# The output projection of an attention by Strassen's seven products, in a three-layer kernel on one Trainium2 core

## The chip, the cores and the metric

The kernel runs on one core of one Trainium2 chip. A core has five engines that work side by side, each through its own list of instructions in a fixed order: TensorE (PE in the profile) multiplies matrices into PSUM, VectorE (DVE) and ScalarE (ACT) do elementwise work, GpSimd (POOL) does some of it too and issues the indirect transfers, SyncE (SP) issues the other transfers. An instruction can wait for semaphores that other engines or transfers raise; what stands behind it in the same list then waits too.

The metric is the device time of one execution in microseconds (us), as the median of several runs. A profiled execution is one run of its own; its time and its span (first to last instruction) are given beside the median.

## The reference

The input is 4 images of 16 x 16 positions with 1024 channels, 1024 tokens in all, in float32. Three layers follow each other, each added to its input:

```
x = x + conv_hybrid(group_norm(x))        # linear attention with relative positions
t = t + attention(layer_norm(t))          # 16 heads of 64, causal, 256 tokens per image
t = t + ffn(layer_norm(t))                # 8 experts of 1024 x 1024, gated by a softmax
```

The part that matters here is the end of the second layer and the start of the third:

```
y = einsum('bhqk,bhkd->bhqd', att, v).transpose(0, 2, 1, 3).reshape(B, T, C)
t = t + einsum('btc,oc->bto', y, W_proj) + b_proj
...
x = layer_norm(t)
gate_logits = softmax(x @ gate_w + gate_b)
weights = gate_logits * (gate_logits >= 0.1), normalised to sum 1
out = sum over e of weights[:, e] * (x @ expert_w[e] + expert_b[e])
```

The projection multiplies 1024 tokens x 1024 channels by a 1024 x 1024 matrix.

## The kernel before

**Tiles and names.** Tokens lie in 8 tiles of 128 rows (NT). A contraction over 1024 channels is 8 matmuls of 128 x 128 stationary by 128 x 512 moving, added up in one PSUM bank; HALF is 512. y_T is the attention's result with channels on the partitions, so its 128-token columns serve as the stationary operand. w_p holds W_proj's transpose in two halves of its output columns, w_p[0] and w_p[1]. xs (named xb in the profile) are the rows of the residual stream; x_rows is where they wait in DRAM while the attention runs.

**The attention's steps.** Heads go in 8 pairs, images in 4 batches: 32 steps (pair, b). In step i the loop turns the softmax of step i - 2 (`turned`, L619, L620), does products of the query and key projection (`project_qk`, L491), multiplies by the values (`values`, L629, L636) and computes the next scores (`scores`: matmuls at L575 into the one PSUM buffer `sc`, then L583 on DVE, the maxima L595, exponentials L597 on ACT, reciprocal L604, multiplication L607 on POOL). From step 28 the projection's first pieces take the place of `project_qk`: `out_at` gives tiles 0 to 2, one half each step.

**Strassen in the kernel.** `project_v`, `project_qk` and the experts' `products` already use the Winograd form with seven products: for 2 x 2 blocks A and B, `sums_of_A` (L150 to L153) forms three sums and, in place of a21, a fourth; three more sums T and one in place of b12 are formed of B. For the attention the sums of B are formed of ln1, which lies in the buffer `big1`; its last reader is the product (7, 3) in step 27.

**The projection.** `project_out(t, j, halfway)` does the 8 matmuls of tile t and half j (L648) and one DVE addition of the bank into xs[t] (L651). After the fourth matmul and after the eighth it calls `halfway`, which starts pieces of the third layer's preparation.

**The gating.** For each tile `stage(n, t)` has four parts: `normalise` (statistics L840 and L842, reciprocal root L131 to L133, the normalised row L846, its transposes L828 on PE, evicted by ACT at L832 and DVE at L834, and a copy by_quarter L850 that SP writes to `rows`); `gate` (matmuls L862 and L866 and a softmax over 8 experts in small DVE instructions, L873 to L885); `place` (matmuls L892 and L893, the position in each expert's list, L900 to L907, entries on POOL or, for the last two tiles, DVE at L915); and `enter` (matmuls L926). The table `after` says behind which half of a piece each stage of each tile is called. `normalise` writes its row into a tile with the tag `ye` (three buffers), by_quarter into the tag `xg` (two).

**The first expert.** `w0` is loaded once the projection's earlier weights are done with. A block under `tc.manual_schedule()`, whose order is the order of the text, begins with `first_sum(0)` and `second_sum(0)` (L1046, L1049: T of 128 x 2048, in a pool `t_pool` of their own), `bias_step` (L1053), the gathers of the first rows (L718, POOL) and a dense product (`weighted`, L739) for the last tile of tokens.

**What sets the order.** Outside that block a scheduler with its own cost estimates orders each engine's list ahead of time; the tile pools decide which buffer a tile takes and so what its first writer has to wait for. PSUM banks come under two tags with three buffers each: `mm` and `tr`; the transposes and the gating's results use `tr`.

Of the kernel before, what the change touches and what calls it, by code (L numbers as in the profile page):

```python
# [32 lines left out]
F32 = mybir.dt.float32  # L33
# [6 lines left out]
P = 128  # L40
# [27 lines left out]
def kernel(  # L68
# [29 lines left out]
    def pool(stack, name, bufs=1, **kw):  # L98
        return stack.enter_context(tc.tile_pool(name=name, bufs=bufs, reuse_waits="tile", **kw))
# [10 lines left out]
    def big_tile(n, name, shape=(NC, TOK)):  # L110
        return big[n].tile([P, *shape], F32, tag="big", name=name)

    def w_tile(name, *parts, home=None):

        w = (home or wpool).tile([P, NC, HALF], F32, tag="w", name=name)
        at = 0
        for part in parts:
            n = part.shape[1]
            nc.sync.dma_start(w[:, :, at : at + n], part.rearrange("(c p) n -> p c n", p=P))
            at += n  # L120
        return w
# [335 lines left out]
    with ExitStack() as attention:  # L457
# [180 lines left out]
        project_v(0)  # L638
        project_v(1)
        y_T = big_tile(0, "y_T")  # L640
        w_p = []

        def project_out(t, j, halfway=lambda: None):
            if not w_p:
                w_p.extend(w_tile(f"w_p{j}", W_projT[:, ts(j, HALF)]) for j in range(2))
            po = mm(f"po{t}_{j}")
            for c in range(NC):
                nc.tensor.matmul(po, y_T[:, c, ts(t, P)], w_p[j][:, c, :], start=(c == 0), stop=(c == NC - 1))  # L648
                if c == NC // 2 - 1:
                    halfway()  # L650
            nc.vector.tensor_add(xs[t][:, ts(j, HALF)], xs[t][:, ts(j, HALF)], po)  # L651
# [11 lines left out]
        units[22].remove((6, 5))  # L663
        units[23] = [(6, 5)]
        units.update({24: [(7, 1), (7, 2), (7, 6)], 25: [(7, 7), (7, 4)], 26: [(6, 3), (7, 5)], 27: [(7, 3)]})
        out_at = {28: (0, 0), 29: (1, 0), 30: (2, 0), 31: (0, 1), 32: (1, 1), 33: (2, 1)}
        for n in order:
            project_qk(0, n)
        soft = {}
        for i in range(len(steps) + 2):  # L670
            if i >= 2:
                s_T = turned(*steps[i - 2], soft.pop(i - 2))
            for unit in units.get(i, ()):
                project_qk(*unit)
            if i == 27:
                sums.close()
                x_pool = pool(x_home, "xb", side="right")
                xs = [x_pool.tile([P, C], F32, tag=f"x{t}", name=f"xb{t}") for t in range(NT)]
                for t in range(NT):
                    nc.sync.dma_start(xs[t], x_rows[ts(t, P), :])  # L680
            if i in out_at:
                project_out(*out_at[i])
            if i >= 2:
                values(*steps[i - 2], s_T)
            if i < len(steps):
                soft[i] = scores(*steps[i])


    left.close()

    rows = dram.tile([TOK, C], F32, name="rows")
    table = rows.rearrange("t (f c) -> (t f) c", f=Q)
# [7 lines left out]


    weights = ExitStack()
    w_even, t_pool = pool(weights, "w_even", 2), pool(weights, "t_pool")

    def half_weights(e, r, home, name="w_e"):

# [25 lines left out]

    def weighted(gate, row_T, w, bias, home, name, between={}):

        y = home.tile([P, C], F32, tag="ye", name=f"{name}_ye", bufs=3)
        for j in range(2):
            pe = mm(f"{name}_pe{j}")
            for c in range(NC):
                nc.tensor.matmul(pe, row_T[:, c, :], w[j][:, c, :], start=(c == 0), stop=(c == NC - 1))  # L739
            between.get(j, lambda: None)()  # L740
            nc.vector.tensor_add(y[:, ts(j, HALF)], pe, bias[:, ts(j, HALF)])
            nc.scalar.mul(y[:, ts(j, HALF)], y[:, ts(j, HALF)], gate)
        return y
# [36 lines left out]
    with ExitStack() as gating:  # L780
# [55 lines left out]
        def normalise(t):  # L836

            stats = small.tile([P, 2, 6], F32, tag="ln_stats", name=f"ln2_stats{t}")
            for j in range(2):
                nc.vector.bn_stats(stats[:, j, :], xs[t][:, ts(j, HALF)])  # L840
            mv = small.tile([P, 2], F32, tag="ln_mv", name=f"ln2_mv{t}")
            nc.vector.bn_aggr(mv, stats)  # L842
            rstd = small.tile([P, 1], F32, tag="ln_rstd", name=f"ln2_rstd{t}")
            inverse_root(rstd, mv[:, 1:2], EPS)
            row = l2w.tile([P, C], F32, tag="ye", name=f"row{t}", bufs=3)
            nc.vector.tensor_scalar(row, xs[t], mv[:, 0:1], rstd, ALU.subtract, ALU.mult)  # L846
            row_T = l2w.tile([P, NC, P], F32, tag="row_T", name=f"row_T{t}", bufs=3)
            transpose_rows(row, row_T, f"row{t}")
            by_quarter = l2w.tile([P, Q, C // Q], F32, tag="xg", name=f"by_quarter{t}")
            nc.scalar.copy(  # L850
                by_quarter.rearrange("p f (c i) -> p c f i", c=NC),
                row.rearrange("p (c f i) -> p c f i", c=NC, f=Q),
            )
            nc.sync.dma_start(rows[ts(t, P), :], by_quarter.rearrange("p f c -> p (f c)"))
            return row_T
# [109 lines left out]
            nc.vector.tensor_copy(add[:, a:b, :], slot[:, a:b, 0, :])  # L965

        w0 = [half_weights(0, r, w_even) for r in range(2)]
        bias0 = expert_bias(0, l2w)


        turned_rows, gated, placed = {}, {}, {}
# [1 line left out]
        def stage(n, t):  # L973
# [8 lines left out]
                enter(t, *placed[t])  # L982


        pieces = [(t, j) for t in range(3, NT) for j in range(2)]
        after = {
            0: (0, 2, 4, 6),
            1: (2, 4, 6, 8),
            2: (4, 6, 8, 10),
            3: (6, 8, 10, 12),  # L990
            4: (9, 11, 13, 15),
            5: (13, 14, 16, 17),
            6: (17, 18, 21, 23),
            7: (20, 22),
        }
        halves = 0

# [5 lines left out]
                        stage(n, t)  # L1003
            halves += 1

        for piece in pieces:
            project_out(*piece, halfway)
            halfway()
        while halves < 24:
            halfway()  # L1010
        read_lists(0, 1, copy_lists(0))

# [29 lines left out]
            return w[e][l][:, 4 * j : 4 * j + 4, :]  # L1042

        def first_sum(e):
            T[e] = [t_pool.tile([P, NC // 2, HALF], F32, tag=f"T{i}", name=f"T{i}_{e}") for i in range(3)]
            nc.vector.tensor_sub(T[e][0], half(e, 0, 1), half(e, 0, 0))  # L1046

        def second_sum(e):
# [9 lines left out]
        def third_sum(e):  # L1058
# [5 lines left out]
                last_rows.append(free[:, NC // 2 : NC // 2 + 2, :].rearrange("p a b -> p (a b)"))  # L1064
            nc.vector.tensor_sub(T3[e], half(e, 0, 1), half(e, 1, 1))

        row = {}
        last = SLOTS // P

# [62 lines left out]
        def left_over(e):  # L1132

            d = e - 1
            between = {0: lambda: (fourth_sum(e), put(e, 1), get(e, 3)), 1: lambda: row_sums(e, 0)}
            get(e, 2)
            y_d, y_e = (l2w.tile([P, C], F32, tag="ye", name=f"left{e}_{i}", bufs=3) for i in range(2))

            for j in range(2):
                bank = (tr if j else mm)(f"left{e}_{j}")  # L1140
                for c in range(NC):
                    a = A[d, last][:, c, :] if j == 0 or c < NC // 2 else A[d, "sum"][:, c - NC // 2, :]
                    for i in range(Q):
                        stationary, of = (a[:, ts(i, 32)], d) if i < Q - 1 else (A[e, last][:, c, 64:LEFT], e)
                        nc.tensor.matmul(  # L1145
                            bank[ts(i, 32), :], stationary, w[of][j][:, c, :], start=(c == 0), stop=(c == NC - 1)
                        )
                between[j]()
                y = y_d[:LEFT, ts(j, HALF)]
# [182 lines left out]
```

## Time and profile before

| what | value |
|---|---|
| median of 3 runs | 1291.41 us (1291.14 to 1291.78) |
| the profiled execution: its time | 1290.33 us |
| the profiled execution: its span | 1288.5 us |
| mean granted PE clock | 0.994 |
| PE busy | 1266.1 us, 98% of the span |
| DVE busy | 670.3 us, 52% |
| ACT busy | 248.7 us, 19% |
| POOL busy | 336.7 us, 26% |
| projection's matmuls, L648 | 647.3 to 789.8 us, 116.1 us busy |
| rows of the projection's result added, L651 | 16 of 128 x 512, 685 ns each |
| half-clock stretches | 304.79 to 308.20, 792.90 to 799.72, 837.27 to 840.68 us |

Lines of the timeline read: start, length, engine, line of the kernel, operation, what is written and read, how many; in brackets the idle time of that engine just before, and what ended it. A matmul in float32 appears as two records, so eight records are four matmuls. Records of PE overlap: a run's length has a tail in which the next one has already begun.

### The profile page before, as it was taken

To read this page: it belongs to the slowest core of one execution; us is meant where nothing else is said; L and a number is where in the kernel's file an instruction comes from. 1 tells how busy PE (TensorE), PEld (TensorE's weight loads), DVE (VectorE), ACT (ScalarE), POOL (GpSimd) and SP (SyncE) were. 2 spreads that over 40 slices of the span, in tenths; PEclk is the share of its full clock that TensorE was granted. 3 is DMA by queue.
4 is the path that set the end of the run, shared out by engine and by line. 5 is a ranking of instruction groups with operands and counts; after the bars stand their busy time and mean duration, and the time that the engine had idled before them with its cause. 6 is when DMAs were issued, how large, how long until landed. Compare 5 with 4: busy or idle time off the path is not lost.

```text
span 1288.5 us, 12902 instructions
## 1 busy us (share of the span) xinstructions
PE 1266.1 (98%) x4838; PEld 676.3 (52%) x4838; DVE 670.3 (52%) x1265; ACT 248.7 (19%) x578; POOL 336.7 (26%) x359
## 2 busy tenths in 40 slices
PE   9999999998999999999999998999999999999998
PEld 5444895787884455555454554444344434433443
DVE  5884210566322555555344745655656565665642
ACT  3300111230000333334223322011111011111110
POOL 0000060230000211222121010553644555263520
PEclk9999999999999999999999998999999999999999
DMA  9020022612202202010323515365667475557442
GB/s 353 4 66 15 3 70 65 243 66 82 66 1 65 66 1 66 1 66 1 112 85 98 198 50 199 95 177 129 157 175 224 99 235 131 160 108 220 98 82 51
DMA packets 60563, 134.58 MB, mean 104 GB/s; under 512 B 5808, under 2 KB 20160, under 8 KB 60496
## 3 DMA queue, kind: packets, MB, share of 16 engines
q1 hardware_dynamic: 47664, 94.32, 20.8%
q0 software_dynamic: 12832, 39.39, 13.9%
q8 instruction: 40, 0.66, 0.2%
q14 instruction: 27, 0.22, 0.1%
HBM read 96.72 MB, written 32.77 MB: 100 GB/s over the span
## 4 chain that ended last, share of the span: by engine, by line
PE 93%; DVE 4%; DMA 1%; POOL 1%; issue 1%; ACT 0%; DVEq 0%; POOLq 0%; ACTq 0%
PE p L1103 29%; PE pqk L491 15%; PE po L648 8%; PE pq L259 7%; PE pv L491 7%; PE left L1145 3%; PE pT L378 3%; PE py L443 2%; PE pk L321 2%; PE pc L342 2%; PE pv L403 2%; PE sc L575 2%; PE pst L619 2%; PE pa L629 2%; PE rest L1159 2%; PE last_pe L1257 1%
## 5 line engine op out<-in xcount | busy, mean ns | idle before, releaser
L718 POOL DMA_INDIRECT w_e_xg<-rows,gather x146 | 156.1, 1069 | 67.4 <-issue 40.5
L1103 PE MATMUL p<-w_e,A 128*128 128x512 f32 x368 | 164.9, 598 | 1.8 <-DVE slot L964 1.8
L607 POOL TENSOR_TENSOR s<-s,total 128x256 f32<-128x256 f32 x64 | 51.6, 827 | 345.3 <-DVE total L604 345.3
L1103 PEld LDWEIGHTS p<-w_e,A 128*128 128x128 f32 x368 | 70.2, 192 | 91.5 <-issue 91.1
L648 PE MATMUL po<-w_p,y_T 128*128 128x512 f32 x256 | 116.1, 598 | 0.0
L1103 PE MATMUL p<-T,S 128*128 128x512 f32 x256 | 112.7, 593 | 0.0
L1109 ACT ACTIVATE y<-y,slot 128x512 f32<-128x512 f32 x64 | 46.0, 722 | 340.6 <-DVE y L1117 185.6
L746 POOL DMA_INDIRECT out_dram<-y,add x32 | 57.0, 1782 | 175.5 <-ACT y L1109 114.2
L259 PE MATMUL pq<-w_q,xn 128*128 128x512 f32 x224 | 99.6, 596 | 1.4 <-DVE q_s L263 1.1
L491 PE MATMUL pqk<-ln,w_qk 128*128 128x512 f32 x192 | 85.0, 592 | 0.0
L1103 PEld LDWEIGHTS p<-T,S 128*128 128x128 f32 x256 | 48.6, 190 | 60.8 <-issue 60.7
L648 PEld LDWEIGHTS po<-w_p,y_T 128*128 128x128 f32 x256 | 46.3, 190 | 49.1 <-issue 48.7
L728 DVE STREAM_TRANSPOSE A<-w_e_xg 128x1024 f32<-128x1024 f32 x32 | 39.6, 1239 | 58.4 <-DMA w_e_xg<-rows,gather 58.4
L259 PEld LDWEIGHTS pq<-w_q,xn 128*128 128x128 f32 x224 | 41.8, 190 | 51.8 <-issue 47.4
L597 ACT ACTIVATE s<-s,top 128x256 f32<-128x256 f32 (+1 forms) x128 | 56.6, 443 | 18.0 <-DVE top L595 18.0
L491 PEld LDWEIGHTS pqk<-ln,w_qk 128*128 128x128 f32 x192 | 35.9, 190 | 42.1 <-issue 41.1
L620 ACT COPY s_T<-pst 128x384 f32<-128x384 f32 x64 | 27.5, 481 | 157.6 <-PE pst L619 157.6
L491 PE MATMUL pqk<-T,S_qk 128*128 128x512 f32 x128 | 57.7, 593 | 0.0
L1103 PE MATMUL p<-w_e,S 128*128 128x512 f32 x128 | 57.5, 592 | 0.0
L1103 PE MATMUL p<-T,A 128*128 128x512 f32 x128 | 57.5, 592 | 0.0
L491 PE MATMUL pv<-w_v,ln 128*128 128x256 f32 x192 | 43.8, 381 | 0.0
L1145 PE MATMUL left<-w_e,one 128*32 128x512 f32 x312 | 41.8, 593 | 0.0
(266 smaller groups left out, 1818.5 us busy)
## 6 DMA issues: line engine op xcount, KB each, us to landing
w_e<-in_expert_w_dram SPq DMA_DIRECT2D x16, 2048.0 KB, 12.4
w_qk<-in_W_attnT_dram SPq DMA_DIRECT2D x8, 1024.0 KB, 5.2
xn<-in_xT_dram SPq DMA_DIRECT2D x8, 512.0 KB, 7.9
x_at<-in_x_dram SPq DMA_DIRECT2D x8, 512.0 KB, 8.0
w_v<-in_W_attnT_dram SPq DMA_DIRECT2D x2, 2048.0 KB
x_rows<-x_at SPq DMA_DIRECT2D x8, 512.0 KB, 2.6
w_p<-in_W_projT_dram SPq DMA_DIRECT2D x2, 2048.0 KB, 7.6
xb<-x_rows SPq DMA_DIRECT2D x8, 512.0 KB, 6.0
```

The source lines that it names most:

```text
L259: nc.tensor.matmul(pq, xn[:, c, ts(t, P)], w_q[kc][:, c, :], start=(c == 0), stop=(c == NC - 1))
L378: nc.tensor.matmul(out_T[:, g, :, :], window[:, kc, :, :].rearrange("p i j -> p (i j)"), q0[:, kc, first : first + n_i, nj, :], start=(kc ...
L491: nc.tensor.matmul(bank, stationary(c), moving(c), start=(c == 0), stop=(c == NC // 2 - 1))
L597: nc.scalar.activation(s[:, h, cols], s[:, h, cols], AF.Exp, bias=top[:, qt, h : h + 1], accum_out=total[:, qt, h : h + 1],)
L607: nc.gpsimd.tensor_mul(s[:, :, cols], s[:, :, cols], total[:, qt, :].unsqueeze(2).to_broadcast([P, 2, (qt + 1) * P]),)
L648: nc.tensor.matmul(po, y_T[:, c, ts(t, P)], w_p[j][:, c, :], start=(c == 0), stop=(c == NC - 1))
L718: nc.gpsimd.indirect_dma_start(out=row[:, g, :], out_offset=None, in_=table[: (TOK - P) * Q, :] if e in SHORT else table, in_offset=bass.I ...
L728: nc.vector.transpose(row_T[:, :, :slots].rearrange("p c (g j) -> p g c j", j=32), row[:, : slots // 32, :].rearrange("p g (c i) -> p g c ...
L746: nc.gpsimd.indirect_dma_start(out=out[: TOK - P, :] if e in SHORT else out, out_offset=bass.IndirectOffsetOnAxis(ap=add[:slots, e, k : k ...
L1103: nc.tensor.matmul(bank, a[:, c, :], b[:, c, :], start=(c == 0), stop=(c == NC // 2 - 1))
L1109: nc.scalar.mul(y[i][:, ts(j, HALF)], y[i][:, ts(j, HALF)], slot[:, e, 1, 2 * pair + i : 2 * pair + i + 1])
L1145: nc.tensor.matmul(bank[ts(i, 32), :], stationary, w[of][j][:, c, :], start=(c == 0), stop=(c == NC - 1))
```

## The change

The projection of the first six tiles is done in three pairs of tiles. A pair's 256 x 1024 block of y is cut into 2 x 2 blocks (tile by half of the contraction), w_p into 2 x 2 blocks (half of the contraction by half of the outputs), and seven products of four matmuls give the four blocks of the result. `out_sums` forms the sums of w_p once, three of them in `big1` (where ln1 was), one in place of b12; `pair_sums` forms a pair's sums of y, with the fourth in place; `project_pair` does one product and its additions into xs. Tiles 6 and 7 keep the eight matmuls per half; as b12 no longer holds the weights, the second half's last four matmuls use `tile_sum`, the sum of both halves of y.

The sums use 15 of the 16 pieces of `big1`; so `big1` is kept to the end (`left.close()` goes), and the experts' T then lie there (`t_e`) instead of in `t_pool`. The tag `ye` gets two buffers for three, and the first expert's bias takes an `xg` buffer. The table `after` is written anew for the new order of pieces.

```diff
-        def project_out(t, j, halfway=lambda: None):
-            if not w_p:
-                w_p.extend(w_tile(f"w_p{j}", W_projT[:, ts(j, HALF)]) for j in range(2))
+        def out_sums():
+            nonlocal t_p, s_p, u_p
+            w_p.append(w_tile("w_p1", W_projT[:, HALF:]))
+            flat = big_tile(1, "out_sums").rearrange("p a b -> p (a b)")
+            t_p = [flat[:, ts(i, 4 * HALF)].rearrange("p (c n) -> p c n", n=HALF) for i in range(3)]
+            s_p = [flat[:, ts(12 + i, HALF)] for i in range(3)]
+            u_p = flat[:, ts(15, HALF)]
+            b11, b12, b21, b22 = (w_p[l][:, 4 * j : 4 * j + 4, :] for j in range(2) for l in range(2))
+            nc.vector.tensor_sub(t_p[0], b12, b11)
+            nc.vector.tensor_sub(t_p[1], b22, t_p[0])
+            nc.vector.tensor_sub(b12, b12, b22)
+            nc.vector.tensor_sub(t_p[2], b21, t_p[1])
...
+        def pair_sums(pair):
+            blocks = (y_T[:, 4 * j : 4 * j + 4, ts(2 * pair + i, P)] for i in range(2) for j in range(2))
+            sums_of_A(*blocks, *(by_tile(a) for a in s_p))
+
+        def tile_sum(t):
+            nc.vector.tensor_add(by_tile(s_p[t % 2 * 2]), y_T[:, :4, ts(t, P)], y_T[:, 4:, ts(t, P)])
+
+        def project_pair(pair, n):
...
+            a, b = {
+                1: (a11, b11),
+                2: (a12, b21),
+                3: (s4, b22),
+                4: (a22, t_p[2]),
+                5: (s1, t_p[0]),
+                6: (s2, t_p[1]),
+                7: (s3, t3),
+            }[n]
+            bank = (tr if n in (3, 5, 6) else mm)(f"po{pair}_{n}")
+            for c in range(NC // 2):
+                nc.tensor.matmul(bank, a[:, c, :], b[:, c, :], start=(c == 0), stop=(c == NC // 2 - 1))
+
+            u2, u3 = u_p, s_p[1]
+            if n == 1:
+                nc.scalar.copy(u2, bank)
+                nc.vector.tensor_add(c11, c11, bank)
+            elif n == 2:
+                nc.vector.tensor_add(c11, c11, bank)
+            elif n == 3:
+                nc.vector.tensor_add(c12, c12, bank)
+            elif n == 6:
+                nc.vector.tensor_add(u2, u2, bank)
+                nc.vector.tensor_add(c12, c12, u2)
+            elif n == 7:
+                nc.vector.tensor_add(u3, u2, bank)
+                nc.vector.tensor_add(c22, c22, u3)
+            elif n == 5:
+                nc.vector.tensor_add(c12, c12, bank)
+                nc.vector.tensor_add(c22, c22, bank)
+            else:
+                nc.vector.tensor_add(c21, c21, bank)
+                nc.vector.tensor_add(c21, c21, u3)
+
+        def project_out(t, j, halfway):
             po = mm(f"po{t}_{j}")
             for c in range(NC):
-                nc.tensor.matmul(po, y_T[:, c, ts(t, P)], w_p[j][:, c, :], start=(c == 0), stop=(c == NC - 1))
+                y = by_tile(s_p[t % 2 * 2])[:, c - 4, :] if j and c >= 4 else y_T[:, c, ts(t, P)]
+                nc.tensor.matmul(po, y, w_p[j][:, c, :], start=(c == 0), stop=(c == NC - 1))
...
-        out_at = {28: (0, 0), 29: (1, 0), 30: (2, 0), 31: (0, 1), 32: (1, 1), 33: (2, 1)}
+        out_order = [(pair, n) for pair in range(3) for n in (1, 2, 3, 6, 7, 5, 4)]
...
+            if i == 25:
+                w_p.append(w_tile("w_p0", W_projT[:, :HALF]))
             if i == 27:
+                out_sums()
                 sums.close()
...
-            if i in out_at:
-                project_out(*out_at[i])
+            out_units = out_order[2 * (i - 28) : 2 * (i - 27)] if i >= 28 else []
+            if i == 28:
+                pair_sums(0)
+            for unit in out_units[:1]:
+                project_pair(*unit)
             if i >= 2:
                 values(*steps[i - 2], s_T)
+            if i == 31:
+                pair_sums(1)
+            for unit in out_units[1:]:
+                project_pair(*unit)
...
-    left.close()
-    w_even, t_pool = pool(weights, "w_even", 2), pool(weights, "t_pool")
+    w_even = pool(weights, "w_even", 2)
...
-        y = home.tile([P, C], F32, tag="ye", name=f"{name}_ye", bufs=3)
+        y = home.tile([P, C], F32, tag="ye", name=f"{name}_ye", bufs=2)
...
-            row = l2w.tile([P, C], F32, tag="ye", name=f"row{t}", bufs=3)
+            row = l2w.tile([P, C], F32, tag="ye", name=f"row{t}", bufs=2)
...
-        bias0 = expert_bias(0, l2w)
...
         after = {
             0: (0, 2, 4, 6),
-            1: (2, 4, 6, 8),
-            2: (4, 6, 8, 10),
-            3: (6, 8, 10, 12),
-            4: (9, 11, 13, 15),
-            5: (13, 14, 16, 17),
-            6: (17, 18, 21, 23),
-            7: (20, 22),
+            1: (1, 3, 5, 7),
+            2: (3, 5, 7, 9),
+            3: (5, 7, 9, 11),
+            4: (9, 11, 13, 14),
+            5: (11, 12, 14, 15),
+            6: (14, 15, 18, 20),
+            7: (17, 19),
         }
...
-        for piece in pieces:
-            project_out(*piece, halfway)
+        for pair, n in out_order[12:]:
+            if (pair, n) == (2, 1):
+                pair_sums(2)
+            project_pair(pair, n)
             halfway()
-        while halves < 24:
+        for t in range(NT - 2, NT):
+            tile_sum(t)
+            for j in range(2):
+                project_out(t, j, halfway)
+                halfway()
+        bias0 = expert_bias(0, l2w, tag="xg", bufs=2)
+        while halves < 21:
             halfway()
...
         def first_sum(e):
-            T[e] = [t_pool.tile([P, NC // 2, HALF], F32, tag=f"T{i}", name=f"T{i}_{e}") for i in range(3)]
+            T[e] = t_e
             nc.vector.tensor_sub(T[e][0], half(e, 0, 1), half(e, 0, 0))
...
+        t_e = big_tile(1, "t_e").rearrange("p a b -> p (a b)")
+        t_e = [t_e[:, ts(i, 4 * HALF)].rearrange("p (c n) -> p c n", n=HALF) for i in range(3)]
```

More of the change, by code (lines that the diff above doesn't have):

```diff
@@ L640 @@
         y_T = big_tile(0, "y_T")
-        w_p = []
-        def project_out(t, j, halfway=lambda: None):
-            if not w_p:
-                w_p.extend(w_tile(f"w_p{j}", W_projT[:, ts(j, HALF)]) for j in range(2))
+        w_p, t_p, s_p, u_p = [], None, None, None
+        def out_sums():
[10 more added lines that the diff above has]
+            nc.vector.tensor_sub(t_p[2], b21, t_p[1])
@@ new lines, in by_tile @@
+        def by_tile(a):
+            return a.rearrange("p (c n) -> p c n", n=P)
+        def pair_sums(pair):
[4 more added lines that the diff above has]
+        def project_pair(pair, n):
+            a11, a12, s3, a22 = (
+                y_T[:, 4 * j : 4 * j + 4, ts(2 * pair + i, P)] for i in range(2) for j in range(2)
+            )
+            b11, t3, b21, b22 = (w_p[l][:, 4 * j : 4 * j + 4, :] for j in range(2) for l in range(2))
+            s1, s2, s4 = (by_tile(a) for a in s_p)
+            c11, c12, c21, c22 = (xs[2 * pair + i][:, ts(l, HALF)] for i in range(2) for l in range(2))
+            a, b = {
[30 more added lines that the diff above has]
+                nc.vector.tensor_add(c21, c21, u3)
@@ L982, in stage @@
                 enter(t, *placed[t])
-        pieces = [(t, j) for t in range(3, NT) for j in range(2)]
         after = {
             0: (0, 2, 4, 6),
-            1: (2, 4, 6, 8),
-            2: (4, 6, 8, 10),
-            3: (6, 8, 10, 12),
-            4: (9, 11, 13, 15),
-            5: (13, 14, 16, 17),
-            6: (17, 18, 21, 23),
-            7: (20, 22),
+            1: (1, 3, 5, 7),
[5 more added lines that the diff above has]
+            7: (17, 19),
         }
@@ L1136, in left_over @@
             get(e, 2)
-            y_d, y_e = (l2w.tile([P, C], F32, tag="ye", name=f"left{e}_{i}", bufs=3) for i in range(2))
+            y_d, y_e = (l2w.tile([P, C], F32, tag="ye", name=f"left{e}_{i}", bufs=2) for i in range(2))
             for j in range(2):
```

## The prediction

> **What bounds the kernel now.** I read the page first (busy time, then the chain that ended last), then the two stages that the change touches, then the places where TensorE (PE) waits.
>
> ```profile
> span 1288.5 us, 12902 instructions
> ...
> PE 1266.1 (98%) x4838; PEld 676.3 (52%) x4838; DVE 670.3 (52%) x1265; ACT 248.7 (19%) x578; POOL 336.7 (26%) x359
> ...
> PE 93%; DVE 4%; DMA 1%; POOL 1%; issue 1%; ACT 0%; DVEq 0%; POOLq 0%; ACTq 0%
> ...
> L648 PE MATMUL po<-w_p,y_T 128*128 128x512 f32 x256 | 116.1, 598 | 0.0
> ```
>
> PE is busy 98% of the span and 93% of the chain, so a PE instruction that goes is time, unless a wait takes its place. L648 is the output projection, with no idle time before it. One matmul shows as two records, so x256 is 128 matmuls.
>
> The next fence is busy time by stage: the end of the attention, the projection with the gating, and, from the third line on, four stretches of 3.41 us. The number after the five engines is the granted PE clock.
>
> ```profile
> 645.00:705.00 60.00, 60.00 (x238) 29.98 (x238) 25.70 (x62) 18.60 (x57) 11.82 (x19) 1.00 0.20 75
> 705.00:790.00 85.00, 83.56 (x453) 42.09 (x452) 50.50 (x200) 26.28 (x36) 7.21 (x12) 1.00 0.32 119
> 833.86:837.27 3.41, 1.46 (x5) 0.93 (x6) 3.09 (x13) 0.00 (x0) 0.00 (x0) 1.00 0.00 0
> 837.27:840.68 3.41, 3.41 (x6) 1.33 (x5) 3.05 (x5) 0.25 (x1) 0.00 (x0) 0.50 0.02 5
> 792.90:796.31 3.41, 2.85 (x20) 2.73 (x20) 1.28 (x5) 1.63 (x2) 0.00 (x0) 0.50 1.04 398
> 796.31:799.72 3.41, 3.41 (x19) 1.21 (x12) 2.25 (x10) 0.00 (x0) 0.00 (x0) 0.50 1.03 389
> ```
>
> The reader is to see two things: VectorE (DVE) is 43% and 59% busy in the first two stages, and a stretch in which PE was busy for 1.46 of 3.41 us is followed by one at half clock. Last, the places where PE or DVE waits, or where the order matters, in order of time:
>
> ```profile
> 645.02 0.69 DVE L567 TENSOR_TENSOR qk<-pqk,U_qk 128x512 f32<-128x512 f32 x1 [0.51 <-PE pqk L491]
> ...
> 646.76 0.96 DVE L583 SCALAR_TENSOR_TENSOR s<-sc,mask 128x768 f32<-128x768 f32 x1 [0.44 <-PE sc L575]
> ...
> 650.16 0.18 DVE L604 RECIPROCAL total<-total 128x4 f32<-128x4 f32 x1 [1.40 <-ACT s L597]
> ...
> 650.51 1.61 POOL L607 TENSOR_TENSOR s<-s,total 128x256 f32<-128x256 f32 x2 [4.21 <-DVE total L604]
> ...
> 655.05 0.92 PE L575 MATMUL sc<-qk 64*128 64x256 f32 x8
> ...
> 706.61 1.09 PE L828 MATMUL row_pt<-ident,row 128*128 128x128 f32 x8 [1.21 <-DVE row L846]
> ...
> 718.93 2.29 DVE L1046 TENSOR_TENSOR T<-w_e,w_e 128x2048 f32<-128x2048 f32 x1 [0.49 <-DMA w_e<-in_expert_w_dram]
> ...
> 721.14 0.15 DVE L883 TENSOR_TENSOR g_top<-g_top,g_fix 128x1 f32<-128x1 f32 x1
> ...
> 781.75 3.60 PE L648 MATMUL po<-w_p,y_T 128*128 128x512 f32 x8
> ...
> 789.81 0.69 DVE L651 TENSOR_TENSOR xb<-xb,po 128x512 f32<-128x512 f32 x1
> ...
> 792.50 0.81 DVE L846 TENSOR_SCALAR row<-xb,ln_mv,ln_rstd 128x1024 f32<-128x1024 f32 x1
> ...
> 793.46 1.94 PE L828 MATMUL row_pt<-ident,row 128*128 128x128 f32 x8 [3.68 <-DVE row L846]
> ```
>
> PE waits 3.68 us for the last tile's normalised row, and 1.21 us for tile 0's.
>
> **1. PE work that goes: -10.3 us.** Before, 8 tiles x 2 halves x 8 = 128 matmuls. After, 3 pairs x 7 products x 4 = 84, and tiles 6 and 7 keep 32: 116. A run of 4 (x8 records) shows 3.60 us with its tail; 16 records issue in 6.97 us (647.28 to 654.25, the next instruction's start), so 4 take 3.44 and the 12 that go 3 x 3.44 = 10.3. All lie on PE's chain. Bounds: 10.0, and 10.9 by the page's busy time (24 x 116.1 / 256).
>
> **2. Sums of the weights in front of a softmax: +4.2 us.** out_sums puts four 128x2048 subtractions on DVE. Their length is L1046's: 2.29, and 2.21 to the next start (718.93 to 721.14). The first overwrites ln1's buffer, so it waits for the last product that reads ln1, which is the one that L567 at 645.02 evicts. In the built program's DVE list stand, in this order: L567, the first sum, one y_T eviction (0.40 to the next start), the other three sums, and only then L583 for the scores that PE computed at 645.7. So L583 moves from 646.76 to 645.71 + 4 x 2.21 + 0.40 = 654.95. Two waits follow on PE. The scores have one PSUM buffer: the next L575, due at 655.05, waits for L583's end at 655.9 (0.9). Then PE's list holds the transposes of those late scores. Before, POOL's first product began 3.75 us after L583; now three more pair sums (L151 to L153, 0.69 each) also stand in front of L604: L583 654.95, L150 655.85, L595 to 657.5, three sums to 659.5, POOL at 659.85, its first block done at 660.5, while PE is free at 656.9: about 3.3 us. Before, the same transposes had 3.5 us in hand. Behind L583 on DVE wait only evictions that have PSUM buffers left. Bounds: 0.9 (only the first wait) and 6 (the next L583, also some 4 us late, adds part of its lateness).
>
> **3. The clock after that wait: +1.5 us.** 833.86 to 837.27 shows that a stretch with 1.9 us of PE idle time costs half the clock in the next 3.41 us. With 0.9 and 3.3 us idle, little more than a score product apart, some stretch has as much wherever its borders lie. Half of 3.41 is 1.7; as part of it can fall in the wait itself I take 1.5, with 0 and 3.4 (two stretches, as at 792.90 and 796.31) as bounds. [...]
>
> **4. First stage of the gating: -1.2 us.** PE waited 1.21 us for tile 0's row, because DVE did 3.7 us of constants (701.96 to 705.66) after the last attention matmul. Now two products, 6.9 us, stand on PE between the two, where 4.6 us stood. Bounds -1.2 and 0.
>
> **5. Evictions and sums on DVE: +0.6 us.** Before, 16 additions of 0.69 (L651). After, 3 x 11 + 4 = 37, three sets of four pair sums and two tile sums of 0.69 each. With the weights' sums the first stage goes from 25.7 to about 49 us (9.1 + 8 x 0.69 + 12 x 0.69 more) of some 65, the second from 50.5 to 56 (4.6 of T goes, 15 x 0.69 comes) of 75: three quarters in both. So the cover is DVE's last quarter and the two sets of PSUM buffers. Laid out with these lengths, one product (pair 1's sixth) waits 0.2 for its sum, and one list matmul 0.4 for POOL. Bounds 0 and 6.3 (0.3 for each of 21 products; rival A). ACT's three copies (L832's 0.59) have room in 18.6 of 60.
>
> **6. The first expert's sums land on the path: +4.2 us.** first_sum(0) and second_sum(0) (L1046, L1049) ran at 718.93 and 721.88 beside PE's work. Now T lies where out_sums lay, and the last half of tile 7's projection still reads a tile sum there. In the built DVE list the first sum stands right behind tile 7's last L651, ahead of its statistics, and the second between the statistics and L846. So the wait at 793.46 grows by 2 x 2.21, less 0.2 of the square root's round trip that the second sum covers. Nothing else is on PE then. The half clock that follows (792.90 to 799.72) stays, with 1.7 either way for where the stretches fall; I take 0. Behind L846, gating, lists and the POOL gathers from 803.01 shift as a block.
>
> **At nothing.** w_p's second half still waits for its buffer (issued 629.6, 7.6 us to landing) and is needed at 645.7. w_e's first loads now wait for the last read of v1 instead of ln1; they are needed 60 us later. The bias load (9.4 us to landing) moves on SP behind tile 6's copy, some 15 us ahead of its use; expert 1's now also waits for the last row's transfer (2.6), with expert 2's weights behind it, which wait for expert 0's products anyway. Two row buffers for three: rows come in pairs some 20 us apart, and a copy takes 1.04. POOL's order of work is unchanged.
>
> **Sum:** -10.3 + 4.2 + 1.5 - 1.2 + 0.6 + 4.2 = -1.0. The profiled execution took 1290.33 (span 1288.5); 1.0 less is 1289.3. The median of the runs, 1291.41, lies 1.1 above it: **1290.4**.
>
> **Rivals.** *A, slower: DVE becomes the bound of the pair products.* Each waits for a bank whose eviction stands in DVE's list behind gating work. For it: three quarters busy in strict order, and three of seven products share their buffers with the transposes and gating results. Against it: 0.3 us of slack at each of the gating's products is what the lengths leave. At 0.3 for each of 21 products, 5.7 more than step 5: 1296.1. It decides from (2.6 + 1.0) / 21 = 0.17 us a product. *B, faster: the clock.* It stays full after step 2's wait (-1.5), and the low stretch after the tail is one, not two (-1.7): 1287.2. For it: 705.24 to 706.61, with 1.21 us idle, stayed at full clock. Against: the row at 833.86. *C: the tail's sums are hidden anyway,* as at 718.93: -4.2, 1286.2; against it stands their place in the list.
>
> **How the numbers follow.** A measurement of this kernel can tell about 0.2% (2.6 us) from no change: 1288.8 to 1294.0. The forecast has 0.56 (own range 1288.4 to 1293.2, from the halves of the bounds of steps 2, 3 and 5), A 0.23, B 0.17, C 0.03, anything else 0.01. Faster: B nearly whole, C and a little of the first, 0.21; slower: A and a little of the first, 0.25; within: 0.54. The range reaches into A to 0.25 us a product (1295.4) and down to B's value: 1287.1 to 1295.4.
>
> **What would show it.** Right: the projection's matmuls take 232 records for 256; DVE's four 2.2 us subtractions at 645 to 655 with L583 behind them, and PE waiting 4 us before the next transposes, with clock 0.50 after it; no wait for tile 0's row; a wait of 7.9 us for tile 7's row with the two T sums in it. Wrong: PE waiting for DVE before pair products (A), clock 1.00 after 660 (B), a tail of 4 us (C).

## The result, and the profile after

The changed kernel takes 1290.83 us (median of 12 runs, 1289.11 to 1293.00) and the kernel before, in 12 runs, 1291.28 us (1289.79 to 1292.66). The ratio is 0.9999, with a 95% interval of 0.9990 to 1.0007: no change that can be measured. The forecast was 1290.4 us and "within 0.2%". The profiled execution took 1290.30 us against 1290.33 before, where the steps summed to -1.0.

So twelve matmuls of 0.86 us are gone and nothing is gained. The interest lies in where they went. First the page of the changed kernel: span, busy time, and shares of the chain that ended last.

```profile
span 1288.3 us, 12901 instructions
...
PE 1259.5 (98%) x4814; PEld 673.2 (52%) x4814; DVE 698.1 (54%) x1304; ACT 245.1 (19%) x577; POOL 335.2 (26%) x359
...
PE 90%; DVE 4%; issue 3%; DMA 2%; POOL 1%; ACT 0%; POOLq 0%; DVEq 0%; ACTq 0%
```

PE has 24 records fewer (4838 to 4814), which are the 12 matmuls. Its busy time fell by only 6.6 us. At half clock a matmul is busy for longer (one of the records of L687, at 661.6 us, takes 1.06 us where most take 0.59), and the changed kernel has more of those, as the clock column below shows.

Next, the waits of PE in the changed kernel, sorted by their sum: total us, times, longest.

```profile
PE row_pt L903 <- DVE row L921: 7.6, 1, 7.6
PE pv L491 <- DVE T L480: 4.0, 1, 4.0
PE pst L619 <- POOL s L607: 3.3, 1, 3.3
PE p L1186 <- DVE slot L1039: 1.8, 1, 1.8
...
PE sc L575 <- DVE s L583: 1.0, 1, 1.0
PE pn L1106 <- DVE U L1198: 0.6, 1, 0.6
```

Before, the first of these was two waits of 3.7 and 1.2 us. Now tile 0's row costs nothing and tile 7's costs 7.6. The waits of 3.3 and 1.0 us are new. They lie together, and the timeline shows why: first DVE around 646 us, then PE (start, us, engine, line, operation, output and inputs, idle time before).

```profile
645.59 0.69 DVE L567 TENSOR_TENSOR qk<-pqk,U_qk 128x512 f32<-128x512 f32 x1 [0.52 <-PE pqk L491]
646.20 2.81 DVE L653 TENSOR_TENSOR out_sums<-w_p,w_p 128x2048 f32<-128x2048 f32 x1
648.93 0.47 DVE L636 TENSOR_SCALAR y_T<-pa,bv 128x256 f32<-128x256 f32 x1
649.32 2.27 DVE L654 TENSOR_TENSOR out_sums<-w_p,out_sums 128x2048 f32<-128x2048 f32 x1
651.52 2.28 DVE L655 TENSOR_TENSOR w_p<-w_p 128x2048 f32<-128x2048 f32 x1
653.72 2.28 DVE L656 TENSOR_TENSOR out_sums<-w_p,out_sums 128x2048 f32<-128x2048 f32 x1
655.93 0.95 DVE L583 SCALAR_TENSOR_TENSOR s<-sc,mask 128x768 f32<-128x768 f32 x1
```

```profile
656.93 0.92 PE L575 MATMUL sc<-qk 64*128 64x256 f32 x8 [1.05 <-DVE s L583]
661.12 0.69 PE L619 MATMUL pst<-ident,s 128*128 128x128 f32 x2 [3.27 <-POOL s L607]
```

The softmax's scaling (L583) stands behind the four sums of the weights. PE first waits 1.05 us for the scores' only bank, and then 3.27 us for transposes of the scores that are late by the sums. Then the same places by stretches of 3.41 us (us, busy time of PE, PEld, DVE, ACT, POOL with counts; the first number after POOL is the granted clock):

```profile
653.69:657.10 3.41, 2.36 (x8) 0.82 (x8) 3.41 (x4) 0.00 (x0) 0.00 (x0) 1.00 0.00 0
657.10:660.52 3.42, 0.75 (x8) 0.51 (x8) 3.42 (x8) 1.86 (x8) 0.07 (x1) 0.98 0.00 0
660.52:663.93 3.41, 2.81 (x7) 1.68 (x8) 3.41 (x7) 0.00 (x0) 1.54 (x2) 0.50 0.00 0
663.93:667.34 3.41, 3.41 (x7) 1.58 (x6) 0.30 (x1) 2.61 (x10) 0.00 (x0) 0.52 0.00 0
667.34:670.75 3.41, 3.41 (x15) 1.55 (x14) 1.26 (x3) 0.00 (x0) 0.74 (x2) 1.00 0.00 0
...
645.00:705.00 60.00, 55.56 (x213) 27.26 (x212) 41.19 (x65) 18.30 (x58) 12.50 (x19) 0.94 0.28 98
705.00:790.00 85.00, 81.75 (x457) 41.35 (x455) 61.93 (x238) 23.47 (x34) 7.19 (x12) 1.00 0.36 134
```

The wait is followed by two stretches at half clock, where the forecast counted little less than one. The last two lines are the stages as a whole: DVE went from 25.7 to 41.2 us and from 50.5 to 61.9. It is busier, but of the pair products only one waits for it, for 0.12 us at 702 us. Last, the tail, DVE and then PE:

```profile
786.79 0.69 DVE L717 TENSOR_TENSOR xb<-xb,po 128x512 f32<-128x512 f32 x1
787.39 0.17 DVE L954 TENSOR_SCALAR g_keep<-listed 128x8 f32<-128x8 f32 x1
787.47 2.29 DVE L1127 TENSOR_TENSOR t_e<-w_e,w_e 128x2048 f32<-128x2048 f32 x1
...
790.85 2.29 DVE L1130 TENSOR_TENSOR t_e<-w_e,t_e 128x2048 f32<-128x2048 f32 x1
...
793.39 0.81 DVE L921 TENSOR_SCALAR row<-xb,ln_mv,ln_rstd 128x1024 f32<-128x1024 f32 x1
```

```profile
794.34 1.94 PE L903 MATMUL row_pt<-ident,row 128*128 128x128 f32 x8 [7.59 <-DVE row L921]
```

The two sums of the first expert's weights run between tile 7's last addition and its row, while PE waits.

The account, from marks in both profiles: from the start of L567 to the end of PE's last projection matmul passed 144.75 us before (645.02 to 789.77) and 141.16 us after (645.59 to 786.75), 3.6 less. In it are -10.3 of matmuls, +4.32 of the two waits, +3.05 of clock (6.82 us at half speed, in which PE was not waiting for 6.09) and -1.21 of tile 0's row. What remains for the evictions and everything else is +0.55. Then the wait for tile 7's row grows by 3.91 (3.68 to 7.59), the half clock behind it costs about what it did (3.0 for 3.1), and the wait at the experts' counts is 0.44 shorter. Ahead of the changed part the kernel was 0.57 later (a wait of 3.97 for 3.51 at 300 us is most of it). That is hardly the change's doing: the profile of e7, an edit of the kernel before, has 3.9 there too, and that of e1, an edit of the changed kernel, has 3.5. By this account PE's last matmul should start 0.3 later than before, and it starts 0.31 later (1282.20 for 1281.89).

### The profile page after: what moved, and what is told of

It is laid out like the page before. It is cut to its first block, busy times and chain, and to the rows that moved or that the text cites. A ratio compares the mean times of both kernels' runs of the same rounds, so it can differ in the third digit from the quotient of the medians.

```text
span 1288.3 us, 12901 instructions
## 1 busy us (share of the span) xinstructions
PE 1259.5 (98%) x4814; PEld 673.2 (52%) x4814; DVE 698.1 (54%) x1304; ACT 245.1 (19%) x577; POOL 335.2 (26%) x359
## 4 chain that ended last, share of the span: by engine, by line
PE 90%; DVE 4%; issue 3%; DMA 2%; POOL 1%; ACT 0%; POOLq 0%; DVEq 0%; ACTq 0%
PE p L1186 29%; PE pqk L491 15%; PE pq L259 7%; PE pv L491 7%; PE po L687 5%; PE left L1228 3%; PE pT L378 3%; PE py L443 2%; PE pk L321 2%; PE pc L342 2%; PE pv L403 2%; PE sc L575 2%; PE pst L619 2%; PE pa L629 2%; PE po L714 2%
## 5 line engine op out<-in xcount | busy, mean ns | idle before, releaser
L1186 PE MATMUL p<-t_e,S 128*128 128x512 f32 x256 | 112.7, 592 | 0.0
L1186 PEld LDWEIGHTS p<-t_e,S 128*128 128x128 f32 x256 | 48.6, 190 | 60.8 <-issue 60.7
L1186 PE MATMUL p<-t_e,A 128*128 128x512 f32 x128 | 57.5, 592 | 0.0
L1186 PEld LDWEIGHTS p<-t_e,A 128*128 128x128 f32 x128 | 24.4, 190 | 30.9 <-issue 30.6
L378 PE MATMUL pT<-q,window 128*128 128x256 f32 (+3 forms) x256 | 40.4, 320 | 0.0
```

Source lines behind the costliest of these rows:

```text
L378: nc.tensor.matmul(out_T[:, g, :, :], window[:, kc, :, :].rearrange("p i j -> p (i j)"), q0[:, kc, first : first + n_i, nj, :], start=(kc ...
L1186: nc.tensor.matmul(bank, a[:, c, :], b[:, c, :], start=(c == 0), stop=(c == NC // 2 - 1))
```

## The experiments

The theory is the prediction's: the removed matmuls are worth their full time, and they are given back at two places where DVE's list puts long sums in front of what PE waits for, and by the clock behind such a wait. The rivals: DVE has become the bound of all pair products (A); the matmuls were worth less than they look; the clock is low for another reason.

**e7: what are the 12 matmuls worth?** The kernel before, with one term in eight left out for six tiles.

```diff
             for c in range(NC):
+                if t < 6 and c == 1:
+                    continue
                 nc.tensor.matmul(po, y_T[:, c, ts(t, P)], w_p[j][:, c, :], ...
```

> The kernel before with the second of the eight terms left out of each half of tiles 0 to 5 of the output projection, which is 12 of its 128 matmuls; that part of the projection is not computed. Theory (step 1): all 12 lie on PE's chain, 12 x 0.86 = 10.3 us less than the kernel before, 1290.9 - 10.3 = 1280.6 us, 1279 to 1282. Rival (with fewer matmuls PE only waits longer for the softmax products, the gating or DVE): 5 us less or smaller, above 1285.9.

Measured: 1280.56 us (5 runs) beside 1291.19 for the kernel before, 10.6 us less by the medians; the ratio is 0.9922 (0.9908 to 0.9935), or 10.1 us. PE's waits are those of the kernel before, but for 0.4 us more at 300 us. The 12 matmuls lie on the path and are worth their 10.3 us; step 1 holds, and some 10 us were really given back.

**e1: the sums in the tail.** The T of the first expert takes the tile of the output weights' sums itself, so it waits only for the products that read those sums, and no longer for the tile sums.

```diff
-        t_e = big_tile(1, "t_e").rearrange("p a b -> p (a b)")
-        t_e = [t_e[:, ts(i, 4 * HALF)].rearrange("p (c n) -> p c n", n=HALF) for i in range(3)]
+        t_e = t_p
```

> The first expert's T sums lie in the very tile that held the sums of the output weights, so that they no longer wait for the last read of the tile sums; nothing else differs from the changed kernel (1290.83 us median, wait for tile 7's row 7.59 us). Theory (step 6: the two 2.29 us sums in front of tile 7's row are that wait's growth): they run beside the projection of tile 6, the wait falls to about 3.7 us, and the kernel takes 3.9 us less than the changed one, 1286.9 us; with one stretch of 3.41 us at half clock more or less, 1285.2 to 1288.6. Rival (tile 7's row is late for its own gating chain or because DVE is full of evictions): the wait stays above 6 us and the gain is below 1.6 us.

Measured: 1287.71 us (10 runs), 3.1 less than the changed kernel; the ratio to before is 0.9973 (0.9964 to 0.9983). It is within its bounds, 0.8 short of the 3.9 expected; its profile has one stretch at half clock more than the changed kernel's, at 833 us. DVE and the wait in its timelines:

```profile
757.18 2.28 DVE L1130 TENSOR_TENSOR out_sums<-w_e,out_sums 128x2048 f32<-128x2048 f32 x1
```

```profile
789.90 1.94 PE L903 MATMUL row_pt<-ident,row 128*128 128x128 f32 x8 [3.68 <-DVE row L921]
```

The second sum now runs at 757 beside the projection, and the wait for tile 7's row is 3.68 us, exactly that of the kernel before. Step 6 holds: the sums alone made the growth of the wait.

**e2: the sums of the weights, spread.** One behind each of four steps of the attention.

```diff
-            nc.vector.tensor_sub(t_p[0], b12, b11)
-            nc.vector.tensor_sub(t_p[1], b22, t_p[0])
-            nc.vector.tensor_sub(b12, b12, b22)
-            nc.vector.tensor_sub(t_p[2], b21, t_p[1])
+            return [(t_p[0], b12, b11), (t_p[1], b22, t_p[0]), (b12, b12, b22), (t_p[2], b21, t_p[1])]
...
             if i < len(steps):
                 soft[i] = scores(*steps[i])
+            if 27 <= i < 31:
+                nc.vector.tensor_sub(*w_sums[i - 27])
```

> The four 128x2048 sums of the output weights are issued one behind each of the steps 27 to 30 in place of four in a row at step 27; nothing else differs from the changed kernel (1290.83 us). Theory (steps 2 and 3): the waits of 1.05 us and 3.27 us before 661 us go, and with them the 6.82 us at half clock, of which PE worked 6.09 us, so 3.05 us: together 7.4 us less, less about 0.7 us of a new short wait for the transposes, 1284 us, with 1282.9 to 1285 as bounds. If the half clock does not hang on these waits: 4.3 us less, 1286.5. Rival A (DVE is the bound of the pair products): the same 9.2 us of sums on DVE between the evictions make the products wait, and less than 2 us is gained, above 1288.8.

Measured: 1285.20 us (median of 9 runs), ratio 0.9969 (0.9954 to 0.9984). The runs fall in two groups, five from 1283.95 to 1285.20 with a mean clock of 0.993 to 0.994, and four from 1288.63 to 1289.15 with 0.988 or 0.989. In the profiled run, which belongs to the first group, the waits of 1.05 and 3.27 us and the half clock behind them are gone. A wait for transposes of 1.74 us, in two parts, is left at 668 us; two of the sums still end up close together on DVE, with only the scaling L583 between them. The mean gain is 3.9 us by the ratios and the first group's 5.6 to 6.9. A mean clock lower by 0.005 over some 1285 us of span is, by the author's estimate, about 12.9 us more at half clock, which can cost up to 6.4 us of time; that is enough for the 4 us between the groups. The median lies 0.2 above its bounds, and the second group at the edge that was given to rival A. The profile is of the first group and shows no wait of a product over 0.12 us; what the other four runs met is told by their clock alone, and e6 below speaks against A.

**e3: both edits.**

> Both edits together. Theory (the losses are two separate places on PE's chain): the gains add, 3.9 + 6.7 = 10.6 us less than the changed kernel, about 1280.2 us, with 1278.5 to 1282; against the kernel before 11 us less, so that nearly all of the 10.3 us of removed matmuls is kept. Rival A: the sums only move the load of DVE from one place to the other, and the two together give less than the larger of them alone.

Measured: 1282.07 us (6 runs, 1280.13 to 1284.29), ratio 0.9927 (0.9914 to 0.9940): 8.8 us less than the changed kernel and faster than with either edit alone, at the upper end of its bounds. The wait of 1.74 us, counted as 0.7, is 1.0 of the 1.8 us that are missing. It stands in the profile as two waits for POOL's part of the softmax:

```profile
667.69 0.33 PE L619 MATMUL pst<-ident,s 128*128 128x128 f32 x1 [0.62 <-POOL s L607]
669.14 0.77 PE L619 MATMUL pst<-ident,s 128*128 128x128 f32 x5 [1.12 <-POOL s L607]
```

The gains add as far as the runs can tell, so the two places are separate.

**e4: the clock alone.** Three matmuls whose bank nobody reads stand in the time that PE waits anyway.

```diff
             if i == 31:
                 pair_sums(1)
+            if i == 28:
+                bank = mm("warm")
+                for c in range(3):
+                    nc.tensor.matmul(bank, ident, w_p[0][:, c, :], start=True, stop=True)
```

> The changed kernel with three 128x512 matmuls more (their bank is never read) ahead of the second product of the first pair, 2.6 us of PE time that lies within the 4.32 us that PE waits for the late softmax, so that no wait of the program's is shorter by it, only filled. Theory of step 3 (idle time of PE drops the clock): PE idles about 1.5 us there in place of 4.3, the 6.8 us at half clock after it do not come, and the kernel takes 3.0 us less than the changed one, 1287.8 us. Rival (the half clock comes from something else, such as the four sums on DVE, or from a wait that is still long enough): no gain, 1290.5 to 1291.5 us, with 0.50 still granted after 660.

Measured: 1287.09 us (6 runs), 3.7 less than the changed kernel with more work on PE; ratio 0.9970 (0.9958 to 0.9981). Its stretches after the wait:

```profile
657.58:661.00 3.42, 2.95 (x13) 1.26 (x11) 3.42 (x7) 1.86 (x8) 0.00 (x0) 1.00 0.00 0
661.00:664.41 3.41, 2.40 (x10) 1.43 (x11) 3.41 (x8) 0.80 (x2) 1.61 (x2) 1.00 0.00 0
664.41:667.82 3.41, 3.41 (x15) 1.54 (x14) 1.96 (x5) 1.93 (x9) 0.00 (x0) 1.00 0.00 0
```

DVE's four sums and the late softmax are all still there; only PE's idle time is shorter (one wait of 1.5 us where 1.05 and 3.27 us stood), and the clock stays at 1.00 where it was 0.50. So the half clock went with the idle time of PE here, and the account's 3.05 us are its price. (The profiled run is the slowest of the six, 1289.12 us: it has one low stretch more at 300 us and one more in the tail than the profile of the changed kernel.)

**e6: how near was rival A?** One more DVE operation of 128x512 for each of the 21 pair products.

```diff
             u2, u3 = u_p, s_p[1]
+            to = {1: c11, 2: c11, 3: c12, 6: c12, 7: c22, 5: c12, 4: c21}[n]
+            nc.vector.tensor_max(to, to, to)
```

> The changed kernel (1290.83 us) with one more DVE operation of 128x512 (the maximum of a piece of the residual with itself, which changes nothing) ahead of the sums of each of the 21 pair products: 21 x 0.69 = 14.5 us more of DVE's time. Theory (step 5: DVE's last quarter and two sets of PSUM buffers are the cover): PE's waits grow by less than 2 us in all, 1290.5 to 1293. Rival A (DVE sets the pace of the products): each product waits for a good part of the 0.69 us, 6 us or more, above 1296.8.

Measured: 1292.24 us (11 runs), 1.4 more than the changed kernel, ratio to before 1.0004 (0.9995 to 1.0013). PE's waits grow by 0.27 us before 661 and by 1.33 us at 703:

```profile
703.80 0.33 PE L619 MATMUL pst<-ident,s 128*128 128x128 f32 x1 [0.66 <-POOL s L607]
704.79 0.77 PE L619 MATMUL pst<-ident,s 128*128 128x128 f32 x5 [0.67 <-POOL s L607]
```

Of 14.5 us of added work on DVE a tenth reached the time, and that through the softmax, not through a product's bank. Rival A is out, with room to spare.

**e5 and e8: the other waits, filled.** e5 adds four unread matmuls ahead of tile 7's row to the kernel with both edits; e8 adds four more at 300 us and two behind the experts' counts.

```diff
+        bank = mm("warm_tail")
+        for c in range(4):
+            nc.tensor.matmul(bank, ident, w_p[0][:, c % NC, :], start=True, stop=True)
         bias0 = expert_bias(0, l2w, tag="xg", bufs=2)
```

> The kernel with both edits (1282.07 us), with four matmuls of 128x512 more behind the last product of the projection, whose bank is never read: 3.44 us of the 3.67 us that PE waits for tile 7's row. Theory (idle time of PE costs clock as well as itself): the 6.82 us at half clock behind that wait (787.20 to 794.02) go, 3.4 us of time, so 1278.7 us, with 1278.0 to 1280.5 as bounds. Rival (the low clock there comes with the change of the work from the projection to the gating, not with the idle time): the same time, 1281.5 to 1283.

> The same as the kernel with both edits and the four matmuls in the wait for tile 7's row, with four more in the 3.9 us that PE waits at 300 us for the sums of the value weights, and two more in the 2.4 us that it waits at the start of the experts' products (827 us). Theory (as there): the half clock behind these two waits goes too, 1.7 to 3.4 us each, less 0.9 us that the four matmuls cost where the order of VectorE's work shifts and 0.6 us for the two: 1276.5 us, 1274.5 to 1278.5. Rival: the low stretches stay or come elsewhere, above 1279.

e5 took 1281.74 us (4 runs: 1280.24, 1280.62 and twice 1282.86), not the 1278.7 expected; by its time alone the rival (1281.5 to 1283) would hold. The profile, of a run at 1282.86, speaks against it: the half clock behind the tail is gone (the clock is full from 673 to 826 us), and from the transposes of tile 7's row to the first expert's first matmul pass 18.05 us for e3's 20.85. But 0.8 us of it is given back at the experts' counts, where PE now waits 1.50 us for 0.67, and the profiled run has a low stretch at 670 us that e3's has not. e8 took 1278.47 us (4 runs), ratio 0.9899 (0.9884 to 0.9914), just within its bounds. The low stretch at 670 is seen by comparing the same wait of 1.74 us in e3 and in e8, first e3, then e8:

```profile
664.32:667.73 3.41, 2.79 (x14) 1.30 (x12) 3.38 (x8) 1.86 (x8) 0.70 (x2) 1.00 0.00 0
667.73:671.14 3.41, 2.29 (x10) 1.38 (x11) 2.33 (x4) 1.47 (x6) 1.35 (x1) 1.00 0.02 5
671.14:674.56 3.42, 3.42 (x15) 1.44 (x14) 1.24 (x3) 1.14 (x6) 1.61 (x2) 1.00 0.00 0
```

```profile
665.09:668.50 3.41, 1.66 (x13) 1.13 (x10) 3.34 (x7) 0.41 (x2) 2.06 (x2) 0.99 0.00 0
668.50:671.91 3.41, 3.41 (x5) 1.35 (x4) 0.19 (x2) 2.19 (x10) 0.84 (x2) 0.51 0.00 0
671.91:675.33 3.42, 3.42 (x15) 1.54 (x14) 1.72 (x3) 0.00 (x0) 0.77 (x1) 1.00 0.00 0
```

The stretches of e8 are laid, to within 0.1 us, on the changes of its clock. In e3 the clock does not change here; its stretches are laid by whole lengths of 3.413 us back from its change at 787.20. So laid, the wait falls into two stretches of e3, with 0.62 and 1.12 us of idle time, and the clock stays at 1.00; in e8 one stretch has 1.75 us of it, and the next one runs at 0.51. That the lie of the stretches makes this difference was not shown.

**e9 and e10: every long wait filled, with the change and without.** e9 is e8 with one matmul more ahead of the wait at 666 us and one more at the counts; e10 is the kernel before with the same matmuls at 300 us, before tile 7's row and at the counts.

> The kernel with both edits and the filled waits at 300 us and before tile 7's row (with two matmuls behind the lists of the experts it took 1278.47 us), with two edits more: one matmul of 128x512 ahead of the fourth product of the first pair (0.86 of the 1.74 us that PE waits there for transposes at 665 us), and one more between the two small matmuls of the experts' counts, ahead of the two. Theory (a stretch of 3.41 us with under 1.4 us of idle time keeps the full clock): the low stretches behind 668 and 825 us go, 1.7 us each, so 1275.5 us, with 1274 to 1277.5 as bounds. Rival (the matmuls added only cost their time, 0.86 each): 1279.5 to 1280.5.

> The kernel before (1291 us) with the same unread matmuls in its waits at 300 us (four), before tile 7's row (four) and at the experts' counts (three); nothing else differs. Theory (clock and projection are separate): it gains what the fills gain by themselves, the half-clock stretches of 3.41, 6.82 and 3.41 us, so 1.7 + 3.4 + 1.7 less some 0.9 us where the order of VectorE's work shifts, 5.9 us, to 1285.1 us, with 1284 to 1287.5 as bounds; the seven products with both edits keep some 9 to 10 us of advance over it. Rival (the fills do nothing for the kernel before): 1290 to 1292.

e9 took 1276.52 us (5 runs, 1276.21 to 1276.73), ratio 0.9890 (0.9875 to 0.9905); e10 took 1286.76 us (8 runs, 1286.31 to 1287.25), ratio 0.9971 (0.9960 to 0.9983). Their mean clocks are 0.999 and 1.000. Both lie within their bounds, though the fills alone gained the kernel before 4.0 us and not the 5.9 expected. With the clock held, the seven products with both edits are worth 10.2 us: what the removed matmuls cost. e9 beats both kernels by some 14 us.

## Why the prediction was right

It was right in the time, in the sign and in the mechanism; one term was too small.

1. *PE work, -10.3:* right. The two lines of the projection (L687, L714) have 168 and 64 records, the 232 that were named, and e7 measured 10.6. (Four matmuls at half of 6.97 would be 3.49 us; the 3.44 is what four more add to a run, 7.03 less 3.60.)
2. *Sums in front of a softmax, +4.2:* right: 1.05 and 3.27 us, in the order named (0.9 and 3.3 were written down). The times worked out there, 660.5 and 656.9, give 3.6 for the second; POOL began 4.52 us after L583 where 4.9 was laid out. L583 began at 655.93 for 654.95 plus the 0.57 that all was late; the rest is the first sum's 2.81 for 2.29.
3. *The clock, +1.5:* right in kind, half of the size. It comes to 3.05 in the profile, within the bounds of 0 and 3.4. The step took one stretch, partly hidden by the wait; in the profiled run there were two: the rest of the wait (0.7 us) lay in the first of them, and a second followed. What the row at 833.86 had shown came again here: PE was busy for a part of the stretch before the drop (0.75 of 3.41 us, and 1.46 in that row).
4. *Tile 0's row, -1.2:* right; that wait is in no line any more.
5. *Evictions, +0.6:* the account leaves 0.55, with 0.12 us ahead of pair 1's sixth product, the one that was named for 0.2; e6 shows that DVE had cover for much more.
6. *The tail, +4.2:* 3.9, with both sums where the built list put them; e1 took them away and got the old wait back.

A fell by e6. B did not come: the clock was low after step 2's wait, and behind the tail for three stretches, the first of which lay wholly in the wait. But its core, that the same wait can have a price in the clock or none, is what e3 and e8 show (1.74 us of wait in both, then a clock of 1.00 and of 0.51). C fell by the timeline. The profiled time came out 1.0 above the sum: the clock's 1.5 more and the 0.57 from ahead of the changed part, less 0.3 at the tail, 0.44 at the counts and 0.5 behind PE's last matmul. That the median came within 0.4 of the forecast is partly luck: the forecast added 1.1 for the distance from the profiled run to the median, and in the changed kernel it was 0.5, which makes up for half of the 1.0. In the range, 0.25 us for each of 21 products is 1295.05 by the way that A was reckoned, not 1295.4, and the own range of 1288.4 to 1293.2 does not follow from the halves of the bounds that are named (they sum to -2.7 and +4.7); neither bears on the outcome.

## What to carry to other kernels

Fewer products on a bound engine paid in full here (10.6 us in e7 for the 10.3 of the matmuls), but do so only if the sums that they need are not put in front of that engine's next input: look for them in the list of the engine that makes them, at the point where they become possible, not where they are written. A buffer that is shared can move a sum that had been hidden onto the path: sharing the very tile instead of a new one in its place was worth 3 us here. And a wait of PE had a second price here, in the clock (3.05 us behind waits of 4.32), so a wait that cannot be removed may be worth filling with matmuls that nobody reads (3.7 us in e4, 4.0 in e10).

## What the hardware showed

*Half clock came behind stretches in which PE idled for long.* In the profiles of the two kernels the clock is low, the time behind PE's last matmul aside, from 304.79 to 308.20, 792.90 to 799.72 and 837.27 to 840.68 us before, and from 305.40 to 308.81, 660.39 to 667.22, 790.10 to 800.34 and 837.88 to 841.29 us after: once, twice or three times 3.41 us. Both spans, from PE's first matmul to its last, were cut into stretches of that length that begin and end at these changes, and PE's idle time was worked out in each. Of the stretches at full clock with 0.8 us or more, nine, with 0.80, 0.81, 0.89, 1.04, 1.05, 1.12, 1.21, 1.42 and 1.92 us, were followed by full clock, and seven, with 1.82, 1.95, 2.04, 2.09, 2.54, 3.13 and 3.34 us, by half clock. So the idle time of a stretch alone does not decide (1.92 us was not followed by half clock, 1.82 us was). At half clock, four with 0.56, 0.72, 0.83 and 3.41 us were followed by another low stretch, and seven without idle time by full clock. Why is not known from these runs.

*Runs with a lower mean clock took longer.* The kernel before ranged from 1286.94 us (mean clock 0.997) to 1293.33 us (0.991) in 13 runs beside e9 and e10; these two, with mean clocks of 0.999 and 1.000, ranged over 0.5 and 0.9 us.

*Two sums on DVE were longer beside a product on POOL.* In the changed kernel the first 128x2048 sum took 2.81 us where POOL's softmax product ran in its first 0.66 us, and in e3 the second took 2.96 where POOL ran for 0.8 of it. Every other 128x2048 sum in the profiles of the two kernels took 2.27 to 2.29 us, and none of them had POOL's product beside it. The excess of 0.5 and 0.7 us is near the overlap. That the one makes the other was not tried.
